# A two-layer graph network on one core: the stores of the layer-1 row table stand later in the sync queue

## The chip, the core and the metric

The kernel runs on one core of a Trainium2 chip. The metric is the device time of one execution in microseconds (us). Of the kernel before, three executions took 780.81, 781.73 and 782.48 us; the median, 781.73 us, is the time before. The profiled execution has a span of 780.7 us.

A core has five engines that run side by side, each through its own list of instructions in order: TensorE (PE in the profile; its weight loads are PEld), VectorE (DVE), ScalarE (ACT), GpSimd (POOL) and SyncE (SP). Plain transfers are issued by SP and ACT, gathers by POOL. SP computes nothing here: its list of transfers is what this text calls the sync queue. An instruction in it that has to wait holds up those after it.

## The reference

The input is a table x of 3327 nodes by 512 features and a sparse weighted adjacency matrix adj, 3327 by 3327. Two layers follow, each added to its input:

```python
# layer 0
h = maximum(layernorm(x), 0)
x = x + adj @ (relu(adj @ (h @ W1) + b1) @ W2) + b2
# layer 1
h = maximum(layernorm(x), 0)
attn_a = sigmoid(concat([adj @ h, h]) @ Wa.T + ba)         # attn_b likewise
scores = s_left[:, None] + s_right[None, :]                # two products of h @ W_sa with a vector
e = where(adj != 0, exp(-leaky_relu(scores, 0.01)), 0)
x_a = (e / (e.sum(1) + 1e-5)) @ (h @ W_sa)
x_b = adj @ (h @ W_gcnb) + b_gcnb
x = x + sigmoid(attn_a * x_a + attn_b * x_b)
```

Here `relu(adj @ (h @ W1) + b1)` has 128 features, everything else 512. All is float32.

## The kernel before

Nodes are padded to 3328 rows, that is NB = 26 blocks of 128. The columns of the transposed adjacency are cut into NCH = 7 chunks: six of 512 and a last one of 256. A tile of adjacency is 128 rows by one chunk, 256 KB.

**First pass** (loop at line 495). For each chunk, 26 tiles of the adjacency are loaded and multiplied with u = h @ W1 (line 511). At the same time DVE finds out which columns of the matrix are not empty for which groups of nodes, and lists are made of them; these let the third stage gather only the rows that it needs.

**Second pass** (loop at line 658). For each chunk c the 26 tiles are loaded again (`load_adj`, line 229, "a" in the profile) and multiplied with g, the 128 hidden features: line 665, "acc_g", two matmul instructions for each tile. The tiles share a pool of 8 buffers, so the load of tile j can be issued once tile j-8 has been used. When a chunk is done, its sum goes to SBUF (line 698), the four blocks of x that belong to it are loaded (line 694, "xb", five buffers) and the bias is added (line 696). What is still to be done for the chunk's four row blocks is the generator `make_h1(c, sT)`, named `late`. It is advanced by one step at every second tile (j = 1, 3, 5, ...) of the next chunk's loop, line 674:

- steps 1 to 4, at tiles 1, 3, 5 and 7, one for each block: "px" (line 580, times W2), the sum with x (line 583), its store for later (line 584, from ACT's queue), layernorm and relu into the row buffer `h = hrow[i % NR]` (line 586), the right-hand score into column 512 of that row (line 587, by `score`, line 559), and the store of the row into `h_dram` from the sync queue (line 588). All of this is traced under `tc.high_priority()`.
- steps 5 to 8, at tiles 9 to 15: the left-hand score of each block (line 593, also line 559).
- step 9, at tile 17: four transposes "pl" that turn these scores (line 597), and copies of them.
- steps 10 to 13, at tiles 19 to 25: `own_logits`, two more row products each (line 566).

`h_dram` is the row table of the change: 3328 rows of 520 floats (512 features, the score, padding), 260 KB for each block. There are NR = 12 row buffers, so a buffer is used again three chunks later. The row buffers are read in place for the 128 nodes of block 0, the hubs: their sums are made directly ("acc_hub", line 624, with "e_hub" made by lines 206 to 213 and 654), from chunk 2 on, beside the tiles. On POOL, gathers of adjacency columns ("ae", line 139) run throughout the pass, paced by its matmuls.

The order of an engine's instructions is not simply that of the text. The framework orders each engine's list by priority among what can go, so that high priority moves an instruction forward, and one whose buffer is free can stand earlier than it is written. The trace shows it: the xb loads are written after a chunk's loop, and some are issued before that loop has begun.

**Third stage** (line 747 on). For each block, rows of `h_dram` are gathered by the lists (line 774), weighted and summed (line 809, "acc"), transposed (line 823, "ptt") and multiplied with the weights (lines 863 and 870, "p_b" and "p_a"). The first of these gathers can run only when all rows of the table have landed. A part after that (from line 970) is skipped unless the lists overflow.

The lines of the text that the change is about:

```python
                    _, last_row[0] = ln_relu(h[:, :D], x1, l0w, f"b{i}")
                    score(i, h[:, :D], 1, h[:, D : D + 1])
                    nc.sync.dma_start(h_dram[i * P : (i + 1) * P, :], h)
```

Of the kernel before, what the change touches and what calls it, by code (L numbers as in the profile page):

```python
# [18 lines left out]
P = 128  # L19
# [27 lines left out]
def kernel(  # L47
# [17 lines left out]
    nc = tc.nc  # L65
# [5 lines left out]
    NCH = len(chunks)  # L71
# [11 lines left out]
    def bank(pool, name):  # L83
        return pool.tile([P, CW], F32, tag="bank", name=name)
# [27 lines left out]
    h_dram = dram.tile([NP, ROW], F32, tag="h_rows", name="h_rows")  # L112
# [17 lines left out]
    NR = 12  # L130
# [3 lines left out]
    hrow = [t[:, k, :] for t in rows for k in range(2)]  # L134
# [52 lines left out]
    def ln_relu(dst, src, pool, name, stats_behind=(), root_behind=(), relu_behind=()):  # L187

        stats = pool.tile([P, 6], F32, tag="bn6", name=f"bn_{name}", bufs=3)
        with queued(*stats_behind):  # L190
            nc.vector.bn_stats(stats, src)
        ln = pool.tile([P, 5], F32, tag="ln5", name=f"ln_{name}", bufs=3)
        nc.vector.bn_aggr(ln[:, 0:2], stats)
        with queued(*root_behind):
            nc.scalar.activation(ln[:, 2:3], ln[:, 1:2], AF.Sqrt, bias=eps)
        nc.vector.reciprocal(ln[:, 3:4], ln[:, 2:3])
        scaled = nc.vector.scalar_tensor_tensor(
            ln[:, 4:5], ln[:, 0:1], -1.0, ln[:, 3:4], op0=ALU.mult, op1=ALU.mult
        )
        with queued(*relu_behind):  # L200
            made = nc.scalar.activation(dst, src, AF.Relu, bias=ln[:, 4:5], scale=ln[:, 3:4])  # L201
        return scaled, made
# [13 lines left out]
    with (  # L216
# [340 lines left out]
        def score(i, h, s, into):  # L557
            junk = l0w.tile([P, D], BF16, tag="junk", name=f"junk_{i}_{s}", bufs=1)
            return nc.vector.scalar_tensor_tensor(  # L559
                junk, h, 1.0, w_rows[:, s, :], op0=ALU.mult, op1=ALU.mult, accum_out=into  # L560
            )

        def own_logits(i, junk):

            for s in range(2):
                nc.vector.scalar_tensor_tensor(
                    junk, hrow[i % NR][:, :D], 1.0, w_own[:, s, :], op0=ALU.mult, op1=ALU.mult,
                    accum_out=node[i][:, 1 + s : 2 + s],
                )
            nc.vector.tensor_tensor(node[i][:, 1:3], node[i][:, 1:3], bab_row, ALU.add)  # L570

        def make_h1(c, sT):

            c0, w = chunks[c]
            blocks = range(c0 // P, (c0 + w) // P)
            for b, i in enumerate(blocks):
                x1 = xs.pop(i)
                with tc.high_priority():
                    px = bank(psB, f"px_{i}")
                    last_row[2] = nc.tensor.matmul(  # L580
                        px, sT[:, b * P : (b + 1) * P], W2_sb, start=True, stop=True
                    )
                    nc.vector.tensor_tensor(x1, px, x1, ALU.add)  # L583
                    nc.scalar.dma_start(x1_dram[i], x1)
                    h = hrow[i % NR]
                    _, last_row[0] = ln_relu(h[:, :D], x1, l0w, f"b{i}")
                    score(i, h[:, :D], 1, h[:, D : D + 1])
                    nc.sync.dma_start(h_dram[i * P : (i + 1) * P, :], h)
                if c:
                    rows_made.add(i)  # L590
                yield
            for i in blocks:
                last_row[1] = score(i, hrow[i % NR][:, :D], 0, node[i][:, 0:1])
                yield
            pl = bank(psB, f"pl_{c}")
            for b in range(w // P):
                nc.tensor.transpose(
                    pl[:, b * P : (b + 1) * P],
                    node[c0 // P + b][:, 0:1].to_broadcast([P, P]),
                    ident,  # L600
                )
            n = w // P
            plv = pl.rearrange("p (b i) -> p b i", i=P)
            nc.scalar.copy(s_left[c][:HALF, :n, :], plv[:HALF, :n, :HALF])
            nc.scalar.copy(s_left[c][HALF:, :n, :], plv[HALF:, :n, HALF:])
            if c == 0:
                nc.scalar.copy(s_hub, pl[:, :P])
            rows_made.update(blocks)
            yield
            for i in blocks:  # L610

                if c < NCH - 2:
                    own_logits(i, l0w.tile([P, D], BF16, tag="junk", name=f"junk_{i}", bufs=1))
                yield
# [43 lines left out]
        for c in range(NCH):  # L658
# [38 lines left out]
            sT = l0w.tile([HID, CW], F32, tag="gT", name=f"sT_{c}")  # L697
            nc.scalar.copy(sT[:, :w], acc[:, :w])
            late = make_h1(c, sT)
        for _ in columns:  # L700
            pass
# [45 lines left out]
    with tc.tile_pool(name="spw", bufs=2) as spw:  # L747
# [170 lines left out]
        for i in range(NB - 2, 1, -1):  # L918
# [7 lines left out]
            b, ty, es = turning  # L926
# [19 lines left out]
        b, ty, es = turning  # L946
# [23 lines left out]
    with tc.If(over > 0):  # L970
        with (
# [25 lines left out]
            for c in range(NCH):  # L997
# [34 lines left out]
                for b in range(w // P):  # L1032
                    i = c0 // P + b
# [63 lines left out]
```

## Time and profile before

| stage | from, us | to, us |
|---|---|---|
| first pass | 0 | 225 |
| second pass | 225 | 432 |
| last rows, hubs, first gathers | 432 | 455 |
| third stage | 455 | 781 |

Engines over the whole span: POOL is busy 489.8 us (63%), ACT 185.5 us (24%); PE and DVE stand in the lines further below. The issues of the sync queue that matter, with the median time from issue to landing: 325 adjacency tiles of 256 KB, 4.0 us; 26 row stores of 260 KB, 4.1 us; 26 xb loads of 256 KB, 5.0 us. Over the span DMA moves 200.15 MB, 256 GB/s on average.

How such pages are read: "<-" names what an instruction waited for, and a number in brackets is the engine's idle time just before. "x4" at the end of a timeline's row counts instructions merged into it. A chain of waits is followed back from the last instruction to whatever released it; it can charge a transfer while the engine that wanted it was still busy with earlier work. A "px to px" window is the time from one chunk's first px matmul to the next one's, and so the pace of the second pass.

### The profile page before, as it was taken

The numbers are of one execution on the slowest core, as the hardware profiler recorded it, in microseconds if no ns is written. First come the engines' busy times: TensorE is split into PE (matmuls) and PEld (weight loads), VectorE is DVE, ScalarE is ACT, GpSimd is POOL, SyncE is SP. The second block draws the span as 40 slices with busy tenths as digits, with TensorE's granted clock in tenths as the row PEclk, the third lists the DMA queues.
The fourth block names the chain that finished last, engine by engine and source line by source line (L and its number), as shares of the span: only waits on it lengthen the run. The fifth ranks groups of instructions, "written<-read, shape, count | busy, mean of one in ns | idle before, by whom it ended". The sixth has DMA issues, their size and how long they took to land.

```text
span 780.7 us, 12235 instructions
## 1 busy us (share of the span) xinstructions
PE 755.4 (97%) x3647; PEld 415.5 (53%) x3647; DVE 517.5 (66%) x1658; ACT 185.5 (24%) x396; POOL 489.8 (63%) x513
## 2 busy tenths in 40 slices
PE   9999989999999999999999999999999999999995
PEld 8775434444544344344446456665665666655453
DVE  6768979999992876759577575555465464644542
ACT  6882000000000331403215212221221221311211
POOL 1400746666777777777773277677777777777720
PEclk9999999999999999999999999999999999999998
DMA  7888899889889999899998578688888888888840
GB/s 241 247 261 262 272 296 289 263 270 293 230 262 288 319 333 336 283 323 318 311 336 266 171 226 242 202 245 255 252 238 253 251 234 260 225 258 229 228 154 32
DMA packets 107099, 200.15 MB, mean 256 GB/s; under 512 B 17009, under 2 KB 30864, under 8 KB 107024
## 3 DMA queue, kind: packets, MB, share of 16 engines
q1 hardware_dynamic: 72800, 124.40, 48.7%
q0 software_dynamic: 25536, 63.74, 29.8%
q10 hardware_dynamic: 8688, 11.15, 4.3%
q8 instruction: 31, 0.51, 0.3%
q14 instruction: 44, 0.36, 0.2%
HBM read 179.39 MB, written 20.55 MB: 256 GB/s over the span
## 4 chain that ended last, share of the span: by engine, by line
PE 82%; DMA 7%; DVE 7%; issue 1%; ACT 1%; POOL 0%; SPq 0%; POOLq 0%; ACTq 0%; DVEq 0%
PE acc_u L511 16%; PE acc_g L665 14%; PE acc L809 13%; PE p_b L863 12%; PE p_a L870 11%; DMA a<-in_adjT_dram 6%; PE ptt L823 3%; PE pu L293 3%; PE acc_hub L624 2%; PE px L580 2%; PE p_list L459 2%; PE pt L285 1%; DVE junk L559 1%; DVE xb L583 1%; PE awake L100 1%
## 5 line engine op out<-in xcount | busy, mean ns | idle before, releaser
L139 POOL DMA_INDIRECT ae<-in_adjT_dram,row_a x228 | 244.2, 1071 | 145.2 <-DVE most L515 49.1
L139 POOL DMA_INDIRECT hr<-h_rows,row_h x140 | 143.5, 1025 | 47.0 <-issue 27.4
L511 PE MATMUL acc_u<-a,rows 128*128 128x512 f32 (+1 forms) x364 | 164.0, 580 | 1.5 <-DMA a<-in_adjT_dram 1.5
L665 PE MATMUL acc_g<-a,g 128*128 128x512 f32 (+1 forms) x364 | 156.4, 570 | 3.6 <-DMA a<-in_adjT_dram 3.4
L139 POOL DMA_INDIRECT rows<-h_rows,row_h x88 | 90.0, 1022 | 50.7 <-DVE e_hub L206 24.2
L515 DVE TENSOR_REDUCE most<-a 128x16 f32<-128x512 f32 (+1 forms) x182 | 111.1, 640 | 7.2 <-DMA a<-in_adjT_dram 6.8
L665 PEld LDWEIGHTS acc_g<-a,g 128*128 128x128 f32 x364 | 68.2, 192 | 80.1 <-issue 62.7
L863 PE MATMUL p_b<-W_g_sb,tyT 128*128 128x257 f32 x416 | 97.1, 386 | 0.8 <-ACT tyT L836 0.5
L870 PE MATMUL p_a<-W_sa_sb,tyT 128*128 128x512 f32 (+2 forms) x216 | 93.5, 577 | 0.0
L863 PEld LDWEIGHTS p_b<-W_g_sb,tyT 128*128 128x128 f32 x416 | 76.6, 189 | 30.8 <-DVE ae L206 7.3
L511 PEld LDWEIGHTS acc_u<-a,rows 128*128 128x128 f32 x364 | 63.9, 192 | 52.3 <-issue 45.8
L838 DVE COPY tyT<-ptt 128x512 f32<-128x512 f32 x51 | 34.9, 686 | 73.6 <-PE ptt L823 73.5
L809 PE MATMUL acc<-hr,ae 64*64 64x512 f32 x560 | 68.0, 607 | 0.0
L870 PEld LDWEIGHTS p_a<-W_sa_sb,tyT 128*128 128x128 f32 x216 | 41.0, 190 | 37.7 <-issue 35.9
L728 ACT ACTIVATE f<-f 128x2 f32<-128x2 f32 x26 | 5.3, 203 | 173.2 <-DVE f L727 145.8
L809 PE MATMUL acc<-rows,ae 64*64 64x512 f32 x352 | 42.5, 594 | 2.5 <-issue 1.8
L809 PEld LDWEIGHTS acc<-hr,ae 64*64 64x64 f32 x560 | 29.8, 136 | 23.4 <-issue 22.9
L302 ACT ACTIVATE gT<-acc_u,b_col 128x512 f32<-128x512 f32 (+1 forms) x7 | 4.6, 656 | 154.8 <-PE acc_u L511 97.9
L696 DVE TENSOR_TENSOR xb<-xb,b_row 128x512 f32<-128x512 f32 x26 | 17.7, 690 | 29.7 <-DMA xb<-in_x_dram 24.1
L559 DVE SCALAR_TENSOR_TENSOR junk<-rows,w_rows 128x512 bf16<-128x512 f32 x52 | 35.7, 687 | 1.9 <-ACT rows L201 0.9
L583 DVE TENSOR_TENSOR xb<-px,xb 128x512 f32<-128x512 f32 x26 | 16.9, 683 | 24.9 <-PE px L580 24.9
L823 PEld LDWEIGHTS ptt<-ident,ty 128*128 128x128 f32 x208 | 24.2, 141 | 14.2 <-issue 12.9
(142 smaller groups left out, 909.9 us busy)
## 6 DMA issues: line engine op xcount, KB each, us to landing
a<-in_adjT_dram SPq DMA_DIRECT2D x325, 256.0 KB, 4.0
h_rows<-rows SPq DMA_DIRECT2D x26, 260.0 KB, 4.1
x<-in_x_dram SPq DMA_DIRECT2D x26, 256.0 KB, 3.4
xb<-in_x_dram SPq DMA_DIRECT2D x26, 256.0 KB, 5.0
x<-xb ACTq DMA_DIRECT2D x26, 256.0 KB, 2.1
x1b<-x SPq DMA_DIRECT2D x26, 256.0 KB, 4.9
out_dram<-va SPq DMA_DIRECT2D x25, 256.0 KB
ae<-in_adjT_dram,row_a POOLq DMA_INDIRECT x228, 4.4
```

Of the source, the lines that this page charges most:

```text
L139: return nc.gpsimd.indirect_dma_start(out=dst, out_offset=None, in_=table, in_offset=bass.IndirectOffsetOnAxis(ap=rows, axis=0), bounds_ch ...
L293: nc.tensor.matmul(pu[:, :HID], hT[:, k, :], W1_sb[:, k, :], start=(k == 0), stop=(k == KD - 1))
L511: added = nc.tensor.matmul(acc[:, :w], u[j], a[:, :w], start=(j == 0), stop=(j == NB - 1))
L515: nc.vector.tensor_reduce(most[:, : w // GW, j], a[:, :w].rearrange("p (b i) -> p b i", i=GW), axis=AX.X, op=ALU.max, apply_absolute_value ...
L559: return nc.vector.scalar_tensor_tensor(junk, h, 1.0, w_rows[:, s, :], op0=ALU.mult, op1=ALU.mult, accum_out=into)
L583: nc.vector.tensor_tensor(x1, px, x1, ALU.add)
L665: added = nc.tensor.matmul(acc[:, :w], g[j], a[:, j % per, :], start=(j == 0), stop=(j == NB - 1))
L809: added = nc.tensor.matmul(taken[i]["acc"][h][q * HALF : (q + 1) * HALF, :], both[half_p, q * n + k, :], taken[i][k0][k][half_p, q, :D], s ...
L823: moved = nc.tensor.transpose(pt[:, k * P : (k + 1) * P], ty[h][:, k * P : (k + 1) * P], ident)
L838: last = nc.vector.tensor_copy(dst, src)
L863: nc.tensor.matmul(p_b[n][:, :WH], tyT[:, k, 0, :], W_g_sb[:, k, n * WH : (n + 1) * WH], start=(k == 0), stop=(k == KD - 1),)
L870: last = nc.tensor.matmul(p_a[:, c0:c1], tyT[:, k, 1, :], W_sa_sb[:, k, c0:c1], start=(k == 0), stop=(k == KD - 1),)
```

## The change

The store of a row block no longer follows the making of the row. It becomes a function `store_row`, called from later steps of `make_h1`: of a chunk's four stores the first two at steps 7 and 8 (tiles 13 and 15), the third at step 9 (tile 17), the last at step 10 (tile 19). It is then outside `tc.high_priority()`. In the last chunk (256 columns, two blocks), which no pass follows, the stores stay where they were. The stores of chunk c stand in the loop of chunk c+1, so the moved ones are those issued during chunks 1 to 6.

It is meant to keep stores of rows that are not yet made from standing in the sync queue ahead of adjacency loads whose buffers are free.

```diff
+        def store_row(i):
+            nc.sync.dma_start(h_dram[i * P : (i + 1) * P, :], hrow[i % NR])
+
         def make_h1(c, sT):
...
                     score(i, h[:, :D], 1, h[:, D : D + 1])
-                    nc.sync.dma_start(h_dram[i * P : (i + 1) * P, :], h)
+                    if c == NCH - 1:
+                        store_row(i)
                 if c:
                     rows_made.add(i)
                 yield
-            for i in blocks:
+
+            unstored = iter(blocks if c < NCH - 1 else ())
+
+            def store_next():
+                for i in unstored:
+                    store_row(i)
+                    break
+
+            for b, i in enumerate(blocks):
                 last_row[1] = score(i, hrow[i % NR][:, :D], 0, node[i][:, 0:1])
+                if b > 1:
+                    store_next()
                 yield
...
             rows_made.update(blocks)
+            store_next()
             yield
             for i in blocks:
+                store_next()
```

## The prediction

> **What bounds the kernel now.** I read the page first. The PE line and the chain of waits say that TensorE sets the time in all stages: PE is busy 97% of the span and has 82% of the chain.
>
> ```profile
> PE 755.4 (97%) x3647; PEld 415.5 (53%) x3647; DVE 517.5 (66%) x1658; ACT 185.5 (24%) x396; POOL 489.8 (63%) x513
> PE 82%; DMA 7%; DVE 7%; issue 1%; ACT 1%; POOL 0%; SPq 0%; POOLq 0%; ACTq 0%; DVEq 0%
> ```
>
> So an edit to the sync queue can gain only where PE waits for what that queue brings, and that has to be read in the second pass, about 225 to 432 us. The queue's own timeline there shows one pattern for each chunk of 512 columns. This is chunk 3 (counted from 0), whose first matmul of the previous chunk's rows (px) starts at 314.18:
>
> ```profile
> 312.66 9.85 SPq L229 DMA_DIRECT2D a<-in_adjT_dram  x7
> 324.08 0.33 SPq L694 DMA_DIRECT2D xb<-in_x_dram  x1
> 324.88 3.07 SPq L588 DMA_DIRECT2D h_rows<-rows  x4
> 328.05 10.49 SPq L229 DMA_DIRECT2D a<-in_adjT_dram  x13
> ```
>
> The stores of line 588 issue about one per 0.8 us, each as its row is made, so the queue is shut from 324.08 to 328.05. Counted on from the chunk before, the seven loads end with tile 11 and the thirteen begin with tile 12. The PE timeline shows the same tile 12: after the eight px matmuls come 6+8+8+2 matmuls of acc_g at two a tile, and then PE waits.
>
> ```profile
> 329.72 1.02 PE L665 MATMUL acc_g<-a,g 128*128 128x512 f32 x2
> 332.76 2.84 PE L665 MATMUL acc_g<-a,g 128*128 128x512 f32 x6 [2.02 <-DMA a<-in_adjT_dram]
> ```
>
> The chain of the second pass charges such a load in every chunk (two shown). Their sum, 22.4 us, is not what can be won: PE works on earlier tiles for most of it.
>
> ```profile
> 328.05 4.67 DMA a<-in_adjT_dram
> 332.76 2.84 PE acc_g L665 x6
> ...
> 361.03 3.98 DMA a<-in_adjT_dram
> 365.05 2.84 PE acc_g L665 x6
> ```
>
> What can be won is the loss of PE's own pace. In the chain four tiles (eight matmuls of acc_g) take 3.43 us, so one takes 0.857; px takes 3.52, pl 0.44, a pair of hub matmuls 0.86. A chunk with six hub pairs needs 26 x 0.857 + 3.52 + 0.44 + 6 x 0.86 = 31.4 us. The windows from px to px, for chunks 1 to 5, say what it took (length, busy times by engine, granted clock, DMA share, GB/s):
>
> ```profile
> 251.25:281.74 30.49, 29.00 (x66) 12.40 (x65) 22.36 (x75) 8.00 (x17) 23.78 (x23) 0.94 0.97 319
> 281.74:314.18 32.44, 31.87 (x77) 13.84 (x77) 22.24 (x76) 8.90 (x17) 25.42 (x24) 1.00 1.01 338
> 314.18:347.89 33.71, 31.69 (x77) 13.92 (x77) 22.33 (x76) 8.90 (x17) 26.70 (x24) 1.00 0.92 307
> 347.89:380.19 32.30, 31.70 (x78) 13.92 (x77) 22.78 (x76) 8.90 (x17) 23.45 (x21) 1.00 0.95 320
> 380.19:412.02 31.83, 31.69 (x80) 14.22 (x79) 22.11 (x72) 8.70 (x16) 23.31 (x22) 1.00 0.98 319
> ```
>
> Chunks 2 to 5 lose 1.05, 2.3, 0.9 and 0.4 us, 4.7 together. Chunk 1 has no hub pairs and needs 26.3, so it loses 4.2; but it has a second cause. There the four pl transposes stand after tile 12 instead of tile 17, and they wait for the row scores:
>
> ```profile
> 265.46 0.32 PE L597 MATMUL pl<-ident,node 128*128 128x128 f32 x1 [0.20 <-DVE junk L559]
> ...
> 267.66 0.47 PE L597 MATMUL pl<-ident,node 128*128 128x128 f32 x1 [0.41 <-DVE junk L559]
> 268.19 13.71 PE L665 MATMUL acc_g<-a,g 128*128 128x512 f32 x28
> ```
>
> The load that they stand beside lands at 268.14 in the chain, the last score at 267.6: two waits lie on top of each other, and taking away one leaves the other.
>
> **What the Trainium skill says.** "DMA: Bandwidth & Descriptors", section on the anatomy of one DMA, says that a semaphore wait is served by the issuing sequencer before dispatch. The trace agrees: a store whose row is unmade costs the transfer engines nothing, but holds the loads behind it for 3.1 us. The same page, section "Where 436 GB/s comes from", gives about 358 GB/s as one core's limit towards HBM; the trace has 338 over chunk 2 and 358 in its busiest stretch looked at (268 to 272 us), so I use it as a ceiling. "TensorE: Matmul & The Clock Gate", Part 1, says that the clock falls to half after an idle window and needs about 3.4 us of activity to return. The trace agrees: after the pl waits the granted clock is 0.61 in 268 to 272 us, and matmuls start 0.85 us apart, not 0.43. That is some 1.5 us of chunk 1's loss.
>
> **The change part by part.** Nothing is added or removed: 26 stores of 260 KB before and after, 0.32 us of queue each, the same bytes. Moved are 24 of them (chunks 0 to 5, so those issued during chunks 1 to 6). In the text the store of block b goes from tile 1+2b to tile 13+2b and loses its high priority; the queue need not follow the text, but in either order the loads of tiles 12 and 13 come before the first store.
>
> In chunks 2 to 5 load 12 then stands right behind the xb load, which itself waits for the first normalized row (324.08 in chunk 3). It issues at about 324.45 instead of 328.05 and lands, by the 4.67 us of the chain, at 329.1; PE wants it at 330.7. The same sum for chunks 2, 4 and 5 gives 295.2 against 298.3, 361.4 against 364.5 and 393.1 against 396.6. So the wait goes, everywhere with 1.6 us or more to spare. I leave some 0.2 us a chunk for what is no DMA wait (the first matmuls of px and a slower one here and there): 4.7 - 0.8 = 3.9 us gained.
>
> At their new place the stores wait for nothing: rows are made by about 328 in chunk 3, while the load of tile 22 cannot issue before tile 14 is done, at about 333. Each takes one slot of 0.4 us in a queue that needs 0.4 us for each 0.86 us tile. Cost 0; what hides it is PE's work on the eight loaded tiles.
>
> Chunk 1: at least 0.2 us is won (268.19 back to the end of pl), if pl stays where it is. At most 4.2 if pl comes after tile 17 (at about 269.3, after the scores). But chunk 1 moves 30.49 x 319 = 9.7 MB, and at 348 GB/s (between the trace's 338 and 358) that takes 28.0 us, which caps the gain at 2.5. I take the middle, 1.4.
>
> In chunk 6 PE is little held by loads (the row chain through DVE and px ends it), and the last two stores stay. The first row gather, at 441.90, is released by DVE e_hub L206, not by a store. 0. The third stage is paced by PE and moves forward whole. No new buffer wait: a row's buffer is reused three chunks later. Sum: 3.9 + 1.4 = 5.3; 781.73 - 5.3 = 776.4.
>
> **Rivals.** (1) Chunk 1 opens wholly: pl moves behind tile 17, the clock never drops, and transfers keep up because some stores slip into chunk 2. Then 4.2 + 4.0 are won: 773.5. For it: the early pl looks like a filler of the very gap that goes. Against: 9.7 MB in 26.3 us is 370 GB/s, above what any chunk shows.
>
> (2) The gap comes back as a transfer limit or at another tile. DMA shares are 0.92 to 1.01, and a chunk of 31.4 us needs 330 GB/s. For it: chunk 2 already runs at 338 and still lost 1 us. Against: chunk 5 took 31.83 at 319, and PE there lost 0.4. Or the stores stay beside tile 12, since the queue's order is not the text's. About 781.2, a gain of 0.5.
>
> (3) Slower. The stores now come near the two xb loads that are issued after tile 24 and feed the next chunk. DVE works in order and already sat 24.1 us in eight waits at the add of line 696. Late rows cost nothing in chunks 2 to 5, where pl does not wait, but chunk 6 is a chain px, DVE, ACT, DVE up to 438 us, and there four stores of some 0.8 us transfer each would push it: +3.3, 785.0. Against: in chunk 5 these xb loads issue at 402.71, over 9 us before px.
>
> **How the numbers follow.** Forecast (775 to 779) 0.62; (1) 0.12; (2) 0.13; (3) 0.13. Faster by over 0.2% is below 780.2: 0.62 + 0.12 + 0.05 from (2) = 0.79. The rest of (2) and a little of (3) make "same" 0.09; slower 0.12. The range leaves out part of (1) below and (3) with the worse half of (2) above: 773.4 to 780.6.
>
> **What would show it.** Right: in the queue's timeline thirteen and more loads run past tile 12 before the first line-588 store, the idle "<-DMA a" before line 665 in chunks 2 to 5 is gone, and px to px is 31.5 to 31.7 us. Chunk 1 between 28 and 30.3, by where pl stands. Wrong: px to px unchanged with stores at tile 12; a new wait near tiles 20 to 25 or at the start of the next chunk; DMA share over 1 with loads of 6 us and more; or chunk 6 longer than 20.0 us. The forecast fails first if another kind of entry, such as the xb load that waits for a row, then shuts the queue as long.

## The result, and the profile after

The changed kernel takes 775.85 us (median of 6 runs, 774.25 to 776.89) against 782.71 us for the kernel before in the same rounds: ratio 0.9909, 95% interval 0.9887 to 0.9931, so 6.9 us less. Line numbers from 573 on are shifted in the changed kernel by 3 to 16: line 665 (acc_g) is 681, the store of line 588 is line 573 in `store_row`, 597 (pl) is 611, 694 (xb) is 710, 583 (the sum after px) is 586, 580 (px) is 583.

First the queue: the timeline of SP in chunk 3 of the changed kernel. Its first px starts at 313.79.

```profile
312.26 9.85 SPq L229 DMA_DIRECT2D a<-in_adjT_dram  x7
322.63 0.33 SPq L710 DMA_DIRECT2D xb<-in_x_dram  x1
323.05 0.38 SPq L229 DMA_DIRECT2D a<-in_adjT_dram  x1
323.52 0.38 SPq L573 DMA_DIRECT2D h_rows<-rows  x1
324.00 0.91 SPq L229 DMA_DIRECT2D a<-in_adjT_dram  x2
325.00 1.24 SPq L573 DMA_DIRECT2D h_rows<-rows  x1
326.34 1.16 SPq L229 DMA_DIRECT2D a<-in_adjT_dram  x2
327.86 0.33 SPq L573 DMA_DIRECT2D h_rows<-rows  x1
328.52 1.10 SPq L229 DMA_DIRECT2D a<-in_adjT_dram  x2
329.89 0.39 SPq L573 DMA_DIRECT2D h_rows<-rows  x1
```

The block of four stores is gone. Right behind the xb load comes one adjacency load, then stores and loads take turns: one store behind each of the loads 13, 15, 17 and 19. Before, all four stood behind load 12, so they are now one, three, five and seven loads later. The second one still waited a little (1.24 us for one entry). A word on the numbers: the first acc_g after px is tile 1, since tile 0 stands ahead of px. So the gap before lay between loads 12 and 13; the prediction calls them 11 and 12. In chunk 6 nothing moved in the queue: before and after, three stores stand ahead of its last load and one behind it (421.43 to 424.25 us before, 417.47 to 420.29 after), so of the 24 stores that the edit moves in the text only 20 changed their place in the queue.

The PE timeline at the same place (columns: start, length, then the group): where the kernel before did one tile after the hub pair and then waited 2.02 us for tile 13, four tiles now follow each other (eight matmuls in 3.60 us).

```profile
328.46 1.02 PE L640 MATMUL acc_hub<-rows,e_hub 128*128 128x512 f32 x2
329.32 3.60 PE L681 MATMUL acc_g<-a,g 128*128 128x512 f32 x8
332.75 1.02 PE L640 MATMUL acc_hub<-rows,a_hub 128*128 128x512 f32 x2
```

The windows from px to px, chunks 1 to 6 (length, busy times of PE, PEld, DVE, ACT, POOL, granted clock, DMA share, GB/s):

```profile
252.88:282.45 29.57, 27.67 (x66) 11.38 (x65) 22.59 (x75) 7.79 (x17) 23.17 (x22) 1.00 1.01 341
282.45:313.79 31.34, 31.34 (x78) 13.90 (x76) 22.31 (x76) 8.79 (x17) 24.64 (x23) 1.00 1.01 339
313.79:345.21 31.42, 31.42 (x77) 13.98 (x77) 22.32 (x76) 8.91 (x17) 24.71 (x23) 1.00 0.98 326
345.21:376.63 31.42, 31.42 (x77) 13.98 (x77) 22.99 (x76) 8.90 (x17) 24.71 (x23) 1.00 0.96 325
376.63:408.06 31.43, 31.43 (x79) 14.37 (x79) 22.26 (x72) 8.70 (x16) 24.50 (x23) 1.00 0.98 322
408.06:428.06 20.00, 19.20 (x72) 12.56 (x71) 14.46 (x46) 9.56 (x17) 4.62 (x5) 1.00 0.74 233
```

In chunks 2 to 5 PE is busy for the whole window: 31.4 us is its own pace, and nothing is left to win there by loading. Chunk 6 keeps its 20.00 us; before, it had

```profile
412.02:432.02 20.00, 19.20 (x72) 12.57 (x71) 14.46 (x46) 9.55 (x17) 4.44 (x5) 1.00 0.72 224
```

Chunk 1 still takes 29.57 us where PE needs 26.3; now its transfers run at 341 GB/s with a share of 1.01. None of its four stores waits in the queue:

```profile
261.41 0.38 SPq L573 DMA_DIRECT2D h_rows<-rows  x1
263.17 0.44 SPq L573 DMA_DIRECT2D h_rows<-rows  x1
265.62 0.33 SPq L573 DMA_DIRECT2D h_rows<-rows  x1
267.62 0.33 SPq L573 DMA_DIRECT2D h_rows<-rows  x1
```

From these two profiles the six chunks give 180.8 - 175.2 = 5.6 us of the 6.9. The spans differ by 7.1; the other 1.5 us are the sum of 1.6 us lost ahead of chunk 1 and 3.1 us won behind chunk 6, where the kernel before had a stretch at half clock (granted clock 0.59 at 732 to 736 us). The 1.6 us lie ahead of the first of these stores, and chunk 1 began anywhere from 248.6 to 252.9 us in the ten profiles taken on the faster chips, with TensorE's instructions up to there in the same order. Whether the 3.1 us belong to the change had to be tried. The page's chain of waits says nothing here: in the changed kernel it is followed back only to 434 us.

### The profile page after: what moved, and what is told of

Its sections match the earlier page's. It is cut to its first block, busy times and chain, and to the rows that moved or that the text cites. A ratio compares the mean times of both kernels' runs of the same rounds, so it can differ in the third digit from the quotient of the medians.

```text
span 773.6 us, 12232 instructions
## 1 busy us (share of the span) xinstructions
PE 752.6 (97%) x3647; PEld 415.1 (54%) x3647; DVE 518.1 (67%) x1658; ACT 185.3 (24%) x396; POOL 488.6 (63%) x513
## 5 line engine op out<-in xcount | busy, mean ns | idle before, releaser
L825 PE MATMUL acc<-hr,ae 64*64 64x512 f32 x560 | 66.3, 593 | 0.0
L886 PEld LDWEIGHTS p_a<-W_sa_sb,tyT 128*128 128x128 f32 x216 | 40.9, 189 | 37.8 <-issue 35.9
L712 DVE TENSOR_TENSOR xb<-xb,b_row 128x512 f32<-128x512 f32 x26 | 17.7, 689 | 26.5 <-DMA xb<-in_x_dram 26.3
```

What stands on the lines that cost most here:

```text
L712: nc.vector.tensor_tensor(xs[i], xs[i], b2_row, ALU.add)
L825: added = nc.tensor.matmul(taken[i]["acc"][h][q * HALF : (q + 1) * HALF, :], both[half_p, q * n + k, :], taken[i][k0][k][half_p, q, :D], s ...
L886: last = nc.tensor.matmul(p_a[:, c0:c1], tyT[:, k, 1, :], W_sa_sb[:, k, c0:c1], start=(k == 0), stop=(k == KD - 1),)
```

## The experiments

Theory A: stores of rows that are not yet made shut the queue, and the loads behind them are issued too late. Rival B: the megabyte of stores beside the loads is what slows the loads. For chunk 1, theory D: its bytes set its time; rivals C (queue waits or the depth of the eight buffers) and E (the early pl). A ratio is to the kernel before on the same chip. The edits are shown against the changed kernel, those of "the priority alone" and "pl late" against the kernel before; "..." stands for lines left out, and the comments are added here.

**The priority alone.** Same step, no high priority:

```diff
-                    nc.sync.dma_start(h_dram[i * P : (i + 1) * P, :], h)
+                nc.sync.dma_start(h_dram[i * P : (i + 1) * P, :], h)     # outside tc.high_priority()
                 if c:
                     rows_made.add(i)
```

> The store keeps its step and loses only its high priority. The planner then puts every instruction of every engine in the same order as in the kernel before, so this is also a second look at that kernel. Theory A (the queue is shut by stores that wait for unmade rows): no change, ratio 1.000 within 0.003, chunk lengths from px to px near 30.5, 32.4, 33.7, 32.3, 31.8 us. Rival P (priority alone is what matters): faster, as the changed kernel. Open: does the third stage show the half-clock stretch near 732 us again; if it does not, that stretch was an accident of one run and the third stage should be some 3 us shorter.

Ratio 0.9995 (0.9974 to 1.0015). The engines work in the order of the kernel before, so this is a second profile of the same work, and an instructive one. Its windows of chunks 1 to 5:

```profile
248.57:277.96 29.39, 27.70 (x65) 11.77 (x65) 22.40 (x75) 8.00 (x17) 22.99 (x22) 1.00 1.00 334
277.96:311.28 33.32, 31.61 (x78) 13.81 (x76) 22.18 (x76) 8.90 (x17) 26.00 (x25) 1.00 0.99 327
311.28:345.36 34.08, 31.69 (x77) 13.89 (x77) 22.38 (x76) 8.90 (x17) 26.76 (x25) 1.00 0.93 300
345.36:378.79 33.43, 31.69 (x77) 13.90 (x77) 22.73 (x76) 8.90 (x17) 24.34 (x22) 1.00 0.93 310
378.79:412.08 33.29, 31.70 (x80) 14.29 (x79) 22.07 (x72) 8.70 (x16) 22.39 (x21) 1.00 0.93 308
```

Chunks 2 to 5 lose 8.5 us here against 31.4 us each, where the first profile showed 4.7, so the chunk lengths of the first did not recur as expected: the length of such a wait varies from one execution to the next, and the profile that the prediction read was a mild one. Chunk 1 takes 29.39 us with a granted clock of 1.00: the same pl waits of 0.41 us, without the stretch at half clock. Neither that stretch nor the one near 732 us recurs, so both were accidents of one execution. The 3 us that were expected from the loss of the second did not show: from the last px to the end it took 347.7 us against 348.7.

**The wait without the bytes.** The store is cut in two. Eight floats of each row wait at the old place; the 512 features go where the change puts them. Edges in the queue hold load 13 behind the small stores, a large store behind the load before it, and the later xb loads at their place.

```diff
-            nc.sync.dma_start(h_dram[i * P : (i + 1) * P, :], hrow[i % NR])
+            with queued(loaded[0]):
+                nc.sync.dma_start(h_dram[i * P : (i + 1) * P, :D], hrow[i % NR][:, :D])
...
+                    else:
+                        waited[0] = nc.sync.dma_start(h_dram[i * P : (i + 1) * P, D:], h[:, D:])
```

> The row stores of chunks 0 to 5 are cut in two. The padding and score (8 floats of each row, 4 KB) are stored at the old place, after load 12, and wait for the row as before; the 512 features (256 KB) go where the change puts them. Theory A (the wait in the queue costs the time): chunks 2 to 5 lose as in the kernel before, 1 to 2 us each, sum about 4.5; total 780 to 783, not faster than before by more than 0.2%. Rival B (the 1 MB of stores beside the adjacency loads costs the time): chunks 2 to 5 at 31.4 us each, total 775 to 777.

Ratio 1.003 (1.0005 to 1.0054): with 4 KB in place of 260 KB at the old place the gain is gone, and a little more. SP's timeline in chunk 3 (px at 315.35) shows the queue shut as before, for the same 3.07 us, and the PE timeline shows a wait behind it:

```profile
324.76 3.07 SPq L597 DMA_DIRECT2D h_rows<-rows  x4
327.93 0.38 SPq L231 DMA_DIRECT2D a<-in_adjT_dram  x1
```

```profile
334.33 1.98 PE L687 MATMUL acc_g<-a,g 128*128 128x512 f32 x4 [1.57 <-DMA a<-in_adjT_dram]
```

The wait stands one tile later than before: load 13 came in time here, and PE waits for load 14, which stands behind load 13 and one large store, as it does in the changed kernel; there it issues 10.2 us after the first px, here 13.5. Chunks 2 to 5 took 33.3, 33.3, 33.1 and 34.0 us.

**The bytes without the wait.** Four full stores at the old place, but of the rows of the chunk before, which have been made for a chunk. Chunk 1 has none, chunk 6 eight.

```diff
+                if 2 <= c < NCH - 1 and j == 13:
+                    for i in range(4 * (c - 2), 4 * (c - 1)):
+                        with queued(loaded[0]):
+                            stored = store_row(i)
+                    with queued(stored):
+                        a = load_adj(j, c, "a2", per)
```

> The other half: four full stores stand together between loads 12 and 13, as in the kernel before, but they are those of the chunk before (rows made a chunk ago), so that they do not wait. Chunk 1 has none, chunk 6 has eight. Theory A: chunks 2 to 5 at 31.4 to 31.6 us, and chunk 1, freed of 1.06 MB, some 2 to 3 us shorter than 29.6; total 772.5 to 775. Rival B: chunks 2 to 5 lose 1 to 2 us each as before, total 778 to 781.

Ratio 0.9878 (0.9851 to 0.9906). The four stores stand together between loads 12 and 13 and take 2.24 us of the queue in chunk 2 and 2.40 in chunk 3, and yet chunks 2 to 4 run at PE's pace (31.43, 31.52 and 31.43 us; chunk 5 took 32.21 and chunk 6, with its eight stores, 20.60). Its windows of chunks 1 to 3:

```profile
249.87:276.16 26.29, 26.29 (x65) 11.72 (x65) 22.06 (x74) 7.79 (x17) 20.50 (x20) 1.00 1.00 336
276.16:307.59 31.43, 31.43 (x78) 13.99 (x77) 22.60 (x78) 8.90 (x17) 24.71 (x23) 1.00 1.01 342
307.59:339.11 31.52, 31.52 (x77) 13.89 (x77) 22.61 (x76) 8.90 (x17) 25.12 (x22) 1.00 0.96 324
```

With the run before it this settles A against B: in chunks 2 to 5 it is the wait, not the bytes. One thing moved along: the planner put the second xb load of a chunk, which waits for a row, from ahead of load 13 to behind load 23. So two waits are gone from that place; what four stores that do not wait cost behind such an xb load was not tried. That the xb load alone costs nothing there, the changed kernel shows. And chunk 1, without its 1.06 MB of stores, runs at PE's pace for the first time.

**The rows one chunk later.**

```diff
-                    if c == NCH - 1:
+                    if c >= NCH - 2:
                         store_row(i)
...
-            unstored = iter(blocks if c < NCH - 1 else ())
+            unstored = iter(range(c0 // P - 4, c0 // P) if 0 < c < NCH - 1 else ())
```

> As the changed kernel, but the stores of chunks 0 to 4 come one chunk later still (row buffers are free for three chunks), spread over the chunk; those of chunk 5 stay at their own steps. Chunk 1 then moves 1.06 MB less. Theory A with chunk 1 limited by transfers at 341 GB/s (10.1 MB in 29.6 us): chunk 1 takes 9.0 MB at 341 GB/s, 26.5 us, a gain of 3 over the changed kernel; chunks 2 to 5 stay at 31.4; total 772 to 774. Rival C (chunk 1's remaining 3.2 us come from a queue wait or from the depth of eight buffers, not from bytes): chunk 1 stays at 29 to 30, total 775 to 777.

Ratio 0.9874 (0.9849 to 0.9899). Chunk 1 took 27.03 us and chunks 3 to 5 31.4, but chunk 2 took 32.52, and the total of 774.7 us fell between the two forecasts. The planner kept only the rows of chunk 0 back: it put their stores together behind load 8 of chunk 2, while later rows were still stored in the loop in which they were made or at the start of the next, behind loads 20, 23, 25 and 1. So eight stores fell into chunk 2:

```profile
278.33:310.85 32.52, 32.19 (x77) 13.56 (x76) 23.20 (x80) 8.90 (x17) 25.21 (x25) 1.00 0.99 341
```

These are 11.1 MB at 341 GB/s, which fits theory D in another chunk.

**The changed kernel again.**

> The changed kernel again, to be compared on one chip with the runs beside it, and to see what of its profile recurs. Expected: ratio 0.991 within 0.003; chunk 1 at 29 to 30 us with PE waiting for adjacency loads in its second half, chunks 2 to 5 at 31.3 to 31.6 us each. From the last px to the end the first profile took 3 us less than that of the kernel before; if that belongs to the change it recurs (below 340.5 us), if it was an accident it lies anywhere between 339.5 and 343.

Ratio 0.9904 (0.9877 to 0.9931). Chunks 1 to 6 took 29.54, 31.34, 31.71, 31.43, 31.42 and 20.00 us. From the last px to the end of the span (some 6 us more than to the end of the work, which the expectation counts) the kernel before took 348.7 us in its first profile and 347.7 in its second, the changed kernel 345.5 and 346.7; the other kernels tried on such chips, whose third stage is the same, took 347.1 to 350.2. So the 3.1 us do not recur, and most of them are chance; that up to 1 us belongs to the change is not excluded.

**pl late, stores as before.**

```diff
-            for b in range(w // P):
-                nc.tensor.transpose(
+            with queued(tile_done[0] if c == 0 else None):     # the matmul of tile 17
+                for b in range(w // P):
+                    nc.tensor.transpose(
```

> The kernel before, with its stores where they were; only the four pl transposes of chunk 1 are held behind tile 17, where the change has them. Theory D (chunk 1 is limited by its bytes, 10.1 MB at 341 GB/s): chunk 1 stays at 29.3 to 30.5 us and the total within 0.2% of before, 0.998 to 1.001. Rival E (the early pl was the second wait, and its removal gives the gain of chunk 1): chunk 1 at 28 or less, total 2 to 3 us below before.

Ratio 1.001 (0.9994 to 1.0026). The PE timeline of chunk 1, with px at 249.65:

```profile
253.19 10.46 PE L667 MATMUL acc_g<-a,g 128*128 128x512 f32 x24
266.06 4.72 PE L667 MATMUL acc_g<-a,g 128*128 128x512 f32 x10 [2.41 <-DMA a<-in_adjT_dram]
270.62 0.60 PE L598 MATMUL pl<-ident,node 128*128 128x128 f32 x4
```

pl no longer waits, and the load of tile 13 alone costs 2.41 us at the same place. Chunk 1 took 29.56 us.

**pl early, stores as changed.** The steps of chunk 1 run closer together up to pl at tile 12; its stores keep their tiles.

```diff
+                with queued(pl_done[0] if c == 1 and j == 13 else None):
+                    added = nc.tensor.matmul(
...
+                if c == 1 and j in (13, 15, 17, 19):
+                    store_row((j - 13) // 2)
+                if c == 1 and j in (8, 10, 12):
+                    next(late)
```

> The changed kernel, with its stores as changed; only the pl transposes of chunk 1 are put back between tiles 12 and 13, where they wait for the row scores. Theory D: the eight buffers fill while PE waits, and the later waits for loads shrink by as much; chunk 1 at 29.3 to 30.5 us (1.5 more if the clock drops), total within 0.2% of the changed kernel, ratio 0.990 to 0.993. Rival E: the gain of chunk 1 goes, plus 2 to 3 us, ratio 0.994 or more.

Ratio 0.991 (0.9885 to 0.9934), as the changed kernel. Now pl waits again (one of its three waits of 0.41 us is shown), and acc_g waits for no load until near the chunk's end:

```profile
264.43 0.32 PE L611 MATMUL pl<-ident,node 128*128 128x128 f32 x1 [0.41 <-DVE junk L559]
...
266.06 11.64 PE L685 MATMUL acc_g<-a,g 128*128 128x512 f32 x26
277.90 1.13 PE L685 MATMUL acc_g<-a,g 128*128 128x512 f32 x2 [0.20 <-DMA a<-in_adjT_dram]
```

Chunk 1 took 29.08 us. So with either wait, with both, or with neither, chunk 1 takes 29.1 to 30.5 us, the longest of these with the half-clock stretch. What the four have in common is the bytes, 9.7 to 10.2 MB.

**One chunk later, spread.** As "one chunk later", with each store held in the queue behind the load of its tile (13, 15, 17 or 19).

```diff
         def store_row(i):
-            nc.sync.dma_start(h_dram[i * P : (i + 1) * P, :], hrow[i % NR])
+            with queued(loaded[0]):
+                nc.sync.dma_start(h_dram[i * P : (i + 1) * P, :], hrow[i % NR])
```

> Stores of chunks 0 to 4 one chunk later, each held in the queue behind the loads of tiles 13, 15, 17 and 19, so that chunk 2 has them spread as the changed kernel does. No store stands in chunk 1. Theory D: chunk 1 at 26.3 to 27 us, chunks 2 to 5 at 31.4 us, chunk 6 at 20.0 to 20.6; sum of chunks 1 to 5 152 to 153 us against 155.2 in the changed kernel, total 2.5 to 3 us below it, ratio 0.986 to 0.988. Rival C (chunk 1's rest is a queue wait or the depth of eight buffers): no gain over the changed kernel, ratio 0.991.

Ratio 0.9871 (0.9843 to 0.9898), the lowest of all, from four runs; the changed kernel on the same chip had 0.9904, but the intervals overlap. The three kernels without stores in chunk 1 agree, at 0.9871 to 0.9878 against 0.9904 to 0.9910 for the changed kernel and "pl early". Its windows of chunks 1 and 2:

```profile
250.08:276.37 26.29, 26.29 (x65) 11.72 (x65) 22.10 (x74) 7.77 (x17) 20.49 (x20) 1.00 1.00 334
276.37:307.79 31.42, 31.42 (x77) 13.98 (x77) 22.60 (x78) 8.80 (x17) 24.81 (x22) 1.00 1.01 340
```

The eight buffers are the same, the loads keep their order, and chunk 1 has PE busy throughout: the depth of the buffers did not set its time. Taking the stores out takes their bytes and their entries out together; but in the changed kernel the four entries waited for nothing (0.33 to 0.44 us each, above), so theory D holds and rival C falls, on these chips. In the median 1.7 us of the 3.3 us won in chunk 1 arrive (774.63 against 776.34); chunks 4 and 5, at 31.8 and 32.0 us in the profile, gave some 1 us back, and where the rest went stays open.

**The two parts alone.** First only the stores issued in chunk 1 are moved, then only the others.

```diff
-                    if c == NCH - 1:
+                    if c > 0:                  # the other kernel: if c in (0, NCH - 1)
                         store_row(i)
-            unstored = iter(blocks if c < NCH - 1 else ())
+            unstored = iter(blocks if c == 0 else ())     # the other: if 0 < c < NCH - 1
```

> One part of the change alone: only the four stores issued in chunk 1 are moved, the others stay ahead of load 13. Theory A with D: chunk 1 at 29.1 to 29.6 us as in the changed kernel, so nothing or up to 1 us gained there (the second profile of the kernel before had 29.4 without the change), chunks 2 to 5 between 32 and 34 us; ratio 0.998 to 1.001. If the prediction's 1.4 us for chunk 1 holds, 0.998.

> The other part alone: the stores issued in chunks 2 to 6 are moved, those of chunk 1 stay. Theory A with D: chunks 2 to 5 at 31.3 to 31.5 us, chunk 1 at 29.4 to 30.5; nearly the whole gain, ratio 0.990 to 0.992. If the prediction's split (3.9 of 5.3 us) holds, 0.994 to 0.995.

> The same kernel as chunk0_rows_only, whose chip took 856 us for the kernel before, with a third stage some 57 us longer; the question is whether the part's share differs on a chip where the kernel before takes about 783. Theory A with D: ratio 0.998 to 1.001, chunk 1 at 29.1 to 29.6 us, chunks 2 to 5 between 32 and 34 us.

> The same kernel as other_rows_only, for the same reason. Theory A with D: ratio 0.990 to 0.992, chunk 1 at 29.4 to 30.5 us, chunks 2 to 5 at 31.3 to 31.5 us each. If the split of the prediction holds (3.9 of 5.3 us), 0.994 to 0.995.

All four runs fell on two chips where the kernel before takes 854 and 856 us, so whether the split is the same on the faster chips stays unanswered. The stores of chunk 1 alone gave 0.9993 (0.9968 to 1.0019) and 1.0012 (0.9993 to 1.0032): nothing. The others alone gave 0.9943 (0.9921 to 0.9966) and 0.9936 (0.9914 to 0.9959), 4.9 and 5.5 us. The forecast of 0.990 to 0.992 was missed; so was that of 29.1 to 30.5 us for chunk 1. In the last run's windows of chunks 1 to 3 chunks 2 and 3 run as on the other chips, while chunk 1 is another matter:

```profile
261.43:297.37 35.94, 31.22 (x65) 12.51 (x65) 22.56 (x75) 7.99 (x17) 24.98 (x23) 0.91 0.84 276
297.37:328.71 31.34, 31.34 (x78) 13.90 (x76) 22.23 (x76) 8.82 (x17) 23.88 (x21) 1.00 1.01 344
328.71:360.13 31.42, 31.42 (x77) 13.97 (x77) 22.39 (x76) 8.90 (x17) 23.95 (x22) 1.00 0.94 314
```

Chunks 2 to 5 took 127.0 and 127.2 us with their stores moved, 134.5 and 132.7 us without: 5.5 to 7.5 us. Chunk 1 took 34.8 and 35.9 us with its stores unmoved, 32.6 and 34.6 with them moved, so on these chips it may cost something to leave them; the times of the part alone do not show it. Its transfers ran at 276 to 310 GB/s with a share of 0.84 to 0.93, so theory D does not explain chunk 1 here, and what holds it stays open. The whole change was not run there.

## Why the prediction was right, and where it was not

The total of 776.4 us came within 0.6 us of 775.85, and that close a fit is in part luck: the forecast gain was 5.3 us and the measured one 6.9, from a time before of 782.71 us where the prediction had 781.73. The mechanism is shown for chunks 2 to 5: the wait in the queue costs the time without the bytes, and the bytes cost nothing there without the wait. Load 13 issues right behind the xb load, as forecast: 9.3 us after the first px of chunk 3, where the prediction's 324.45 means 10.3. But two terms of the sum were mis-sized in opposite directions.

*Chunks 2 to 5, 3.9 us.* Measured 4.7 (130.3 us less 125.6) in the first pair of profiles and 8.2 in the second (134.1 against 125.9, on two chips), some 6.5 in the mean; "pl late", whose stores in these chunks are those of the kernel before, gives 5.9 on the chip of the second (131.8 against 125.9). Two errors make it up. The 0.2 us a chunk set aside for what is no load wait were not lost: the changed chunks take 31.34 to 31.43 us, which is the sum of the rows, not 31.5 to 31.7. And the loss was read from one execution; the second one lost nearly twice as much.

*Chunk 1, 1.4 us.* The first pair shows 0.9 us, but 1.5 us of its loss before was the half-clock stretch, which the second profile does not have: 29.39 us before against 29.54 after. The part alone gave nothing on the slower chips. That the two waits lie on top of each other was right, and "pl late" and "pl early" show it from both sides. What the step missed is that a third limit lay under both. It did name it, but capped the chunk at 28.0 us with 348 GB/s; at the 334 to 344 GB/s that these profiles show, 10 MB take 29.1 to 29.9 us, which is what was measured, and the cap leaves no gain.

*Where the stores go.* "At their new place the stores wait for nothing", with loads up to tile 22 ahead of them, was wrong, and its sign, thirteen and more loads ahead of the first store, did not come: one load stands there, they follow loads 13 to 19, and one of them waited about a microsecond. It cost nothing: that store had three loads ahead of it, and PE was busy for the whole chunk. The claim that the first store has loads 12 and 13 ahead of it holds for one load, 13 in the true count.

*Chunk 6, the third stage.* The number was right, 20.00 us before and after. But the four stores issued in chunk 6, which the prediction counts as moved, stayed where they were in the queue, so its reason was not put to the test. In the third stage nothing moved beyond what runs differ by.

*The rivals.* (1), chunk 1 wholly opened, was ruled out by its bytes, as argued against it: 370 GB/s did not appear. (2) was wrong for chunk 2, which runs at 339 GB/s in 31.34 us; a higher share of DMA was no new wait. Its sign, a share over 1 with loads of 6 us and more, did show in chunk 1 (1.01, loads of up to 7.0 us in the changed kernel), where the bytes are the limit. (3) did not happen: the xb loads kept their place, and chunk 6 its length; since its stores did not move, the cost that (3) gives them was not tested.

*What was taken from the Trainium skill.* "DMA: Bandwidth & Descriptors", section on the anatomy of one DMA, has the wait served by the issuing sequencer, and "the wait without the bytes" bears it out: 3.07 us of shut queue for 4 KB stores. The 358 GB/s of its section "Where 436 GB/s comes from" were not reached over any chunk, where 344 is the highest, but passed over 4 us (375 GB/s at 366 to 370 us of the kernel before), so as a ceiling they fit neither; the measurement decides. The half clock of "TensorE: Matmul & The Clock Gate", Part 1, is seen in one execution and not in the next with the same waits; the prediction counted it as a fixed part of chunk 1's loss. The idle window that the page names as its cause is not in the trace either: in the 3.4 us ahead of 268.19 PE was busy for 1.92, and no wait was longer than 0.41 us.

## What to carry to other kernels

An entry of a transfer queue that waits for something unmade costs what the entries behind it lose, whatever its own size: put it behind the loads that keep the matrix engine fed. Here one load ahead of the first store, and three ahead of the one that still waited, were enough. Before sizing such a gain, count what the engine's own rows sum to in the stretch, look at the loss in more than one execution, and divide the bytes of the stretch by a rate that the trace has held over as long a time; if that is already the length of the stretch, taking away waits in it brings nothing, and only moving bytes out of it does.

## What the runs showed of the hardware

Reads and writes together were held at 334 to 344 GB/s over chunks of 26 to 32 us at a DMA share of 1.00 to 1.02, while 4 us could show 375. The same order of instructions had waits for loads in chunks 2 to 5 of 4.7 us in one execution and 8.5 us in another. And two chips took 854 and 856 us for the kernel that others run in 783 to 785: most of that lies behind the last px (404 to 407 us to the end of the span against some 347), in the stage of the row gathers, where transfers moved 192 GB/s on one of them against 225 in the changed kernel's second profile. Why transfers are slower there stays open.
